# Side work of an attention block cut into smaller TensorE pieces, and the softmax denominators started earlier

## The chip, the cores and the metric

The kernel runs on one core of one Trainium2 chip. The metric is the device time of one execution in microseconds (us); each kernel's time is the median of its runs. The profile is one execution of the same program on the same kind of chip. TensorE is PE (matmuls) and PEld (its weight loads), VectorE is DVE, ScalarE is ACT, GpSimd is POOL, SyncE is SP.

## The reference

Eight frames of 2048 nodes with 256 channels go through one masked attention block with eight heads of 32 channels, two residual layer norms, a feed-forward layer, and an outer residual layer norm. All is float32.

```python
qkv = einsum('fnc,ck->fnk', x, w_qkv);  q, k, v = split(qkv, 3)      # 8 heads of 32
scores = einsum('fnhd,fmhd->fhnm', q, k) / sqrt(32)
attn = softmax(where(adj > 0, scores, -1e9), axis=-1)
t = einsum('fhnm,fmhd->fnhd', attn, v)
y = layernorm(x + t) * g1 + b1
z = layernorm(y + relu(y @ w1 + b1s) @ w2 + b2) * g2 + b2n
out = layernorm(x + z)                                              # x: the block's input
```

## The kernel before

**The tiling.** Scores are computed transposed: keys lie on the 128 partitions, queries along the row. Four heads make a group `g`, 512 queries a chunk `qc`, 128 keys a block `mb`. One *item* is (frame, chunk, group, block): four heads of 128 keys by 512 queries. A frame has 4 x 2 x 16 = 128 items, the kernel 1024. A run of 16 items (all blocks of one chunk and group) is called a *round* here.

**One item.** `scores` (L207) makes four matmuls of 32 rows that run side by side (L215) into two PSUM pairs out of three; two VectorE adds (L218) put the mask on them and leave them in SBUF as a tile `p` of 128 x 2048; `exponentials` (L221) is one ScalarE instruction in place (L222); `values` (L226) makes four matmuls of 32 columns side by side (L234) that add to one PSUM bank over the 16 blocks. The main loop (L513 to L540) is unrolled: at step t it emits first the side work that is due (`advance`, L428), then the exponentials of item t+1, the scores of item t+2 (`LEAD = 2`), the values of item t, and `add_up` of item t. This is TensorE's program order: side work, scores, values.

**The sums of the exponentials.** The softmax denominators need the sum of 16 `p` tiles. `add_up` (L249) does most of it off TensorE. `POOLED` names seven blocks that GpSimd adds into the first one (six adds, L256). `MOVED` names two chains of four blocks; each is added into the chain's first tile by a 1 MiB accumulating DMA (L253), which GpSimd issues. `ALONE` is a block that stays as it is. That leaves four tiles, and `denominator` (L280) multiplies each by ones on TensorE (L292): 4 heads side by side for each tile, all four tiles adding to one bank. It starts `SUM = 4` steps after the round's last item. Then the bank is copied, transposed (L299) and inverted.

**The side work.** Everything but scores and values is written as generators in a list `fill` that is sorted by due step: `turn` (transposes of x and the query projection), `project` (key and value projection through `channels`, L169, and the matmuls of L197), `denominator`, `outcome` (the division and the accumulating load of the residual), `tail` (L333: layer norms `norm`, L259, and `feed_forward`, L386). Two of the eight PSUM banks belong to neither score pair; one of them holds the running values, the other is for side work. A generator yields `BANK` before each use of that bank, a positive number to wait that many steps, and `INPUTS`, `TURNED` or `ROOM` to wait for a buffer. `advance(t, 1)` gives out one bank per step, in the order of the due steps; it isn't called at a round's first block. A job that got the bank emits all matmuls of the bank at once: 4 records for a projection of 128 x 512 (each float32 matmul shows as two records), 16 for a value projection, 16 for two tiles of `denominator`.

Of the kernel before, what the change touches and what calls it, by code (L numbers as in the profile page):

```python
# [26 lines left out]

SUM_MIN = 1e-25
SUM_MAX = 1e19
BANK, TURNED, ROOM, INPUTS = -1, -2, -3, -10  # L30

MASKED = -57344.0
CODE = -5.0
# [22 lines left out]
def fast_path(ctx, tc, cst, x, adj, out, RS):  # L56
# [20 lines left out]
    ctx.enter_context(tc.manual_schedule())  # L77

    ident, identb, wqkv, w1s, w2s = cst["ident"], cst["identb"], cst["wqkv"], cst["w1s"], cst["w2s"]
    state = {"pair": 0, "side": None, "turn": 0, "turned": False, "tails": 0}  # L80

    def score_pair():
        i = state["pair"]
# [57 lines left out]

    def queries(f, c, xT):
        for g in range(2):
            yield BANK
            QT[f, c, g] = channels(qp, "qT", xT, g * P)

    def turn_rows(xc, xT):
        for a in range(2):
# [17 lines left out]
        yield from queries(f, c, xT)  # L166
        give(xT)

    def channels(pool, name, xT, k0):  # L169
        ps = bank()  # L170
        for a in range(2):
            nc.tensor.matmul(ps, wqkv[:, a, k0:k0 + P], xT[:, a, :], start=(a == 0), stop=(a == 1))  # L172
        t = pool.tile([P, CH], F32, name=name)
        nc.scalar.copy(t, ps)
        return t

    def reload(f, c):
        while (f, c) not in XT:
# [7 lines left out]
    def project(f, c, g, xT=None):  # L186
        if xT is None:
            xT = yield from reload(f, c)
            while len(KT) < (2 * f + g) * NCK + c:
                yield 1  # L190
        yield BANK
        KT[f, c, g] = channels(kp, "kT", xT, C + g * P)
        yield BANK
        ps = bank()
        for j in range(TPC):
            for a in range(2):
                nc.tensor.matmul(ps[:, j * P:(j + 1) * P], xT[:, a, j * P:(j + 1) * P],  # L197
                                 wqkv[:, a, 2 * C + g * P:2 * C + (g + 1) * P], start=(a == 0), stop=(a == 1))
        v = vp.tile([P, TPC, P], F32, name="v")
        nc.scalar.copy(v, ps.rearrange("p (j c) -> p j c", c=P))  # L200
        V[f, c, g] = v
        give(xT)
# [36 lines left out]

    POOLED = (0, 3, 6, 8, 11, 13, 15)
    MOVED = ((1, 4, 7, 10), (2, 5, 9, 12))
    ALONE = 14

    ENDED = (13, 15)
    SUM = 4

    def add_up(item):  # L249
        f, qc, g, mb = item  # L250
# [8 lines left out]
    def norm(t):  # L259
        mv = small.tile([P, TPC, nc.vector.BN_AGGR_DIM], F32, name="mv")  # L260
        for j in range(TPC):
            st = small.tile([P, nc.vector.BN_STATS_DIM], F32, name="st")
            nc.vector.bn_stats(st, t[:, j, :])  # L263
            nc.vector.bn_aggr(mv[:, j, :], st)
            yield 1
        rs = small.tile([P, TPC], F32, name="rs")
        nc.gpsimd.tensor_scalar(rs, mv[:, :, 1], EPS, 1.0, op0=ALU.add, op1=ALU.mult)
        nc.gpsimd.tensor_tensor(rs, rs, cst["mhalf"], ALU.pow)  # L268
        nb = small.tile([P, TPC], F32, name="nb")
        nc.gpsimd.tensor_tensor(nb, mv[:, :, 0], rs, ALU.mult)  # L270
        nc.gpsimd.tensor_scalar(nb, nb, -1.0, 1.0, op0=ALU.mult, op1=ALU.mult)  # L271
        yield 2
        for j in range(TPC):
            nc.scalar.activation(t[:, j, :], t[:, j, :], AF.Identity, bias=nb[:, j:j + 1], scale=rs[:, j:j + 1])  # L274
            yield 1

    def rows(v):
        return v[:, None, :].to_broadcast([P, TPC, C])

    def denominator(f, qc, g):  # L280
        grp = (f, qc, g)
        terms = [PT.pop((f, qc, g, ALONE))] + [PT.pop((f, qc, g, chain[0])) for chain in MOVED + (POOLED,)]
        if (f, qc, g) == items[-1][:3]:
            terms[3:3] = [PT.pop((f, qc, g, b)) for b in ENDED]
        yield BANK
        ps = bank()
        for n, term in enumerate(terms):
            if n == 2:
                yield BANK
            for h in range(4):  # L290
                r = D * h
                nc.tensor.matmul(ps[r:r + D, :], cst["ones"], term[:, h, :], start=(n == 0), stop=(n == len(terms) - 1))  # L292
        dT = op.tile([P, CH], F32, name="dT")
        nc.scalar.copy(dT, ps)  # L294
        yield 1
        yield BANK
        ps = bank()
        for j in range(TPC):
            nc.tensor.transpose(ps[:, j * P:(j + 1) * P], dT[:, j::TPC], ident)  # L299
        if g == 0:  # L300
            RC[f, qc] = op.tile([P, TPC, H], F32, name="rc")
        rc = RC[f, qc]
        den = ps.rearrange("p (j c) -> p j c", c=P)[:, :, ::D]
        nc.vector.reciprocal(rc[:, :, 4 * g:4 * g + 4], den)
        nc.vector.tensor_tensor(RS[:, 0], RS[:, 0], den, ALU.add)
        nc.vector.tensor_tensor(RS[:, 1], RS[:, 1], den, ALU.min)
        if g == 1:
            begin = items.index((f, qc, g, LAST)) + SUM + 2
            start(begin, outcome(f, qc) if (f, qc) != (F - 1, NCK - 1) else finish(f, qc), begin)

    def outcome(f, qc):
        yield ROOM
        state["tails"] += 1
        xin = x[f, qc * CH:(qc + 1) * CH, :].rearrange("(p j) c -> p j c", p=P)
        y = yp.tile([P, TPC, C], F32, name="y")
        yield from divide(f, qc, y)
        nc.gpsimd.dma_start(y, xin, accum_op=ALU.add)
        begin = items.index((f, qc, 1, LAST)) + SUM + 2
        start(begin + 10, tail(f, qc, y, xin), begin + 26)

    def divide(f, qc, y):
        rc = RC.pop((f, qc))
# [43 lines left out]
                nc.scalar.activation(t[:, h + j, :], t[:, h + j, :], AF.Identity, bias=nb[:, j:j + 1], scale=rs[:, j:j + 1])  # L366

    def finish(f, qc):
        y = yp.tile([P, TPC, C], F32, name="y")
        xr, xb = state["rows"], take([P, TPC, C], F32)  # L370
        yield from divide(f, qc, y)
        nc.vector.tensor_tensor(y, y, xr, ALU.add)
        norm_halves(y)
        nc.vector.tensor_tensor(xb, xr, rows(cst["be2r"]), ALU.add)
        yield from feed_forward(y)
        z = y
        norm_halves(z)
        for h in range(0, TPC, 2):
            nc.vector.tensor_tensor(z[:, h:h + 2], z[:, h:h + 2], rows(cst["g2r"])[:, h:h + 2], ALU.mult)
            nc.vector.tensor_tensor(z[:, h:h + 2], z[:, h:h + 2], xb[:, h:h + 2], ALU.add)  # L380
        norm_halves(z)
        dst = out[f, qc * CH:(qc + 1) * CH, :].rearrange("(p j) c -> p j c", p=P)
        for h in range(0, TPC, 2):
            nc.sync.dma_start(dst[:, h:h + 2], z[:, h:h + 2])

    def feed_forward(y):  # L386
# [14 lines left out]
        for d in range(2):  # L401
            yield BANK
            ps = bank()
            for a in range(2):
                nc.tensor.matmul(ps, w1s[:, a, d * P:(d + 1) * P], yT[:, a, :], start=(a == 0), stop=(a == 1))  # L405
            nc.scalar.activation(hT[:, d, :], ps, AF.Relu, bias=cst["b1s"][:, d:d + 1], scale=1.0)
        state["turned"] = False
# [2 lines left out]
        for jj in range(0, TPC, 2):  # L410
            yield BANK
            ps = bank()
            for j in range(jj, jj + 2):
                for d in range(2):
                    nc.tensor.matmul(ps[:, (j - jj) * C:(j - jj + 1) * C], hT[:, d, j * P:(j + 1) * P], w2s[:, d, :],  # L415
                                     start=(d == 0), stop=(d == 1))
            nc.vector.tensor_tensor(z[:, jj:jj + 2, :], ps.rearrange("p (b c) -> p b c", c=C), z[:, jj:jj + 2, :], ALU.add)
# [7 lines left out]

    def advance(t, banks):  # L428
        inputs = True
        for e in list(fill):  # L430
            while e[0] <= t:
                if e[2] == BANK:
                    if not banks:
                        break
                    banks -= 1
                elif e[2] < INPUTS:
                    inputs = inputs and not any(u is not None for u in live[:INPUTS - e[2]])
                    if not inputs:
                        break
                elif e[2] == TURNED and state["turned"] or e[2] == ROOM and state["tails"] == 2:  # L440
                    break
                e[2] = next(e[1], None)
                if e[2] is None:
                    fill.remove(e)
                    break
                if e[2] > 0:
                    e[0] = t + e[2]

    items = [(f, qc, g, mb) for f in range(F) for qc in range(NCK) for g in range(2) for mb in range(MB)]
    LEAD = 2  # L450

# [61 lines left out]
    for t, (f, qc, g, mb) in enumerate(items):  # L513
# [3 lines left out]
            load_mask(f + (qc + 1) // NCK, (qc + 1) % NCK, mb // 2)  # L517
        if f + 1 < F:
            for what, *which in NEXT.get((2 * qc + g, mb), []):
                due = t + MB // 2 if what is turn else items.index((f + 1, 0, which[1], which[0] * TPC)) - LEAD - 1  # L520
                start(t, what(f + 1, *which), due)
        if t == len(items) - MB // 2:
            state["rows"] = take([P, TPC, C], F32)
            nc.sync.dma_start(state["rows"], x[f, qc * CH:(qc + 1) * CH, :].rearrange("(p j) c -> p j c", p=P))
        if mb:
            advance(t, 1)

        if t + 1 < len(items):
            exponentials(items[t + 1])
        if t + LEAD < len(items):  # L530
            nf, _, ng, nmb = items[t + LEAD]
            t0 = t
            while (nf, nmb // TPC, ng) not in V:
                advance(t0, 1)
                t0 += 1
            scores(items[t + LEAD])
        values(items[t])
        add_up(items[t])
        if mb == LAST:
            start(t + SUM, denominator(f, qc, g), t)  # L540
    t = len(items)
    state["side"] = None
    while fill:
        t += 1
        advance(t, 1)


@with_exitstack
# [233 lines left out]
```

## Time and profile before

The median is 3436.56 us (3432.72 to 3441.2); the profiled execution spans 3439.1 us at a granted TensorE clock of 0.99.

| stage | us | what runs |
|---|---|---|
| up to the first exponential | 59.7 | loads, masks, first projections |
| frame 0 | 442.2 | with the rest of the mask work |
| frames 1 to 6 | 414.2 to 419.6 each | steady |
| frame 7 | 382.3 | no next frame to project |
| after the last exponential | 57 | last denominators, last tail |

A frame is counted here from its first exponential to the next frame's. Divided by 128 items, a steady frame takes 3.25 us for an item. In the page, engines that are busy side by side each count fully; the row of a group gives the busy time, the mean of one instruction, and the idle time just before it with what ended it. A PE record's length is modelled and neighbours overlap, so distances from start to start are the better measure of what a matmul costs.

### The profile page before, as it was taken

Reading aid. Unit: us, or ns where it says so; the run is one execution under the profiler, and the core shown is the slowest. Engines: PE = TensorE matmul, PEld = TensorE weight load, DVE = VectorE, ACT = ScalarE, POOL = GpSimd, SP = SyncE. Lnnn points to the kernel's source line nnn. Section 1 sums busy time; section 2 is a strip of 40 time slices with the busy share of each in tenths; the row PEclk is TensorE's granted clock in tenths of the full one; section 3 lists DMA queues with packets and bytes.
Section 4 is the critical chain, followed back from the end, with each engine's and each line's share of the span. In section 5 each row is a group of like instructions: output and inputs, shape, how many; then the busy total and the mean of one; then the engine's idle time right before and its main releaser. Section 6 shows DMA issues by size and latency. Waiting matters only on the chain. (4 is left out here: it accounts for less than half of the span.)

```text
span 3439.1 us, 54435 instructions
## 1 busy us (share of the span) xinstructions
PE 3179.1 (92%) x22036; PEld 1038.5 (30%) x22036; DVE 2731.0 (79%) x3203; ACT 2426.5 (71%) x1937; POOL 2586.7 (75%) x1357
## 2 busy tenths in 40 slices
PE   6989999999999999999999999999999999998995
PEld 5222332223322233222332323223332223322222
DVE  4788768887788877888788887888768887689885
ACT  3677767776677767777677776777767777677774
POOL 0577768887688776888678876787777877788885
PEclk8999999999999999999999999999999999999998
DMA  8678768778678777778777777687776787777774
GB/s 309 149 156 173 173 161 174 158 159 200 142 167 184 154 180 153 163 172 181 170 154 170 161 175 178 141 180 172 164 179 140 160 187 167 169 158 154 151 162 99
DMA packets 149298, 575.99 MB, mean 167 GB/s; under 512 B 14608, under 2 KB 67344, under 8 KB 99888
## 3 DMA queue, kind: packets, MB, share of 16 engines
q0 software_dynamic: 64560, 435.85, 63.2%
q1 hardware_dynamic: 83664, 135.30, 11.4%
q8 instruction: 174, 2.85, 0.3%
q10 hardware_dynamic: 816, 1.31, 0.1%
q14 instruction: 84, 0.69, 0.1%
HBM read 131.99 MB, written 37.75 MB: 49 GB/s over the span
## 5 line engine op out<-in xcount | busy, mean ns | idle before, releaser
L218 DVE TENSOR_TENSOR p<-s,mask 128x1024 f32<-128x1024 f32 x2048 | 2410.0, 1219 | 568.5 <-PE s L215 343.9
L222 ACT ACTIVATE p<-p 128x2048 f32<-128x2048 f32 x1024 | 1956.6, 1911 | 484.6 <-DVE p L218 371.2
L256 POOL TENSOR_TENSOR p<-p 128x2048 f32<-128x2048 f32 x382 | 1851.8, 4898 | 385.9 <-ACT p L222 383.4
L215 PE MATMUL s<-qT,kT 32*128 32x512 f32 x8192 | 1169.8, 641 | 184.9 <-DVE p L218 174.6
L234 PE MATMUL x<-p,v 128*32 128x512 f32 x8192 | 1091.8, 605 | 2.3 <-ACT p L222 2.3
L253 POOL DMA_DIRECT2D p<-p x384 | 385.6, 1024 | 376.0 <-DMA p<-p 188.4
L215 PEld LDWEIGHTS s<-qT,kT 32*128 32x128 f32 x8192 | 320.5, 183 | 822.3 <-DVE p L218 756.2
L234 PEld LDWEIGHTS x<-p,v 128*32 128x32 f32 x8192 | 161.1, 108 | 780.1 <-issue 211.5
L172 PE MATMUL x<-in,wqkv 128*128 128x512 f32 x472 | 235.2, 621 | 14.7 <-DMA in<-xd 14.1
L292 PE MATMUL x<-p,ones 128*32 128x512 f32 x2064 | 244.9, 592 | 1.9 <-DMA p<-p 1.9
L274 ACT ACTIVATE y<-y,nb,rs 128x256 f32<-128x256 f32 x372 | 219.0, 590 | 7.1 <-POOL nb L271 7.1
L263 DVE BATCH_NORM_STATS2 st<-y 128x6 f32<-128x256 f32 x372 | 155.4, 418 | 0.0
L172 PEld LDWEIGHTS x<-in,wqkv 128*128 128x128 f32 x472 | 80.2, 189 | 170.9 <-issue 112.7
L294 ACT COPY dT<-x 128x512 f32<-128x512 f32 x64 | 37.4, 585 | 126.3 <-PE x L292 126.3
L415 PE MATMUL x<-w2s,hT 128*128 128x256 f32 x504 | 125.5, 392 | 0.1
L405 PE MATMUL x<-turned,w1s 128*128 128x512 f32 x248 | 123.0, 618 | 0.0
L197 PEld LDWEIGHTS x<-wqkv,in 128*128 128x128 f32 x896 | 104.2, 191 | 47.0 <-issue 41.1
L197 PE MATMUL x<-wqkv,in 128*128 128x128 f32 x896 | 114.9, 281 | 0.0
L292 PEld LDWEIGHTS x<-p,ones 128*32 128x32 f32 x2064 | 66.8, 110 | 156.4 <-issue 151.0
L415 PEld LDWEIGHTS x<-w2s,hT 128*128 128x128 f32 x504 | 90.6, 189 | 62.0 <-issue 50.3
L268 POOL TENSOR_TENSOR rs<-rs,mhalf 128x4 f32<-128x4 f32 x93 | 96.2, 1035 | 7.8
L200 ACT COPY v<-x 128x512 f32<-128x512 f32 x58 | 33.9, 585 | 93.6 <-PE x L197 93.6
(114 smaller groups left out, 1467.6 us busy)
## 6 DMA issues: line engine op xcount, KB each, us to landing
p<-p POOLq DMA_DIRECT2D x384, 1024.0 KB, 10.1
mask<-md SPq DMA_DIRECT2D x248, 128.0 KB, 6.2
y<-in_x_dram POOLq DMA_DIRECT2D x62, 512.0 KB, 6.1
in<-xd SPq DMA_DIRECT2D x59, 512.0 KB, 10.9
p<-in_adj_dram SPq DMA_DIRECT2D x16, 1024.0 KB, 9.6
out_dram<-y SPq DMA_DIRECT2D x31, 512.0 KB, 6.4
in<-in_x_dram SPq DMA_DIRECT2D x29, 512.0 KB, 10.4
xd<-in SPq DMA_DIRECT2D x28, 512.0 KB, 9.2
```

Source lines behind the costliest of these rows:

```text
L172: nc.tensor.matmul(ps, wqkv[:, a, k0:k0 + P], xT[:, a, :], start=(a == 0), stop=(a == 1))
L197: nc.tensor.matmul(ps[:, j * P:(j + 1) * P], xT[:, a, j * P:(j + 1) * P], wqkv[:, a, 2 * C + g * P:2 * C + (g + 1) * P], start=(a == 0), s ...
L215: nc.tensor.matmul(ps2[half][:, j, :], KT[f, mb // TPC, g][r:r + D, (mb % TPC) * P:(mb % TPC + 1) * P], QT[f, qc, g][r:r + D, :], start=Tr ...
L218: nc.vector.tensor_tensor(pt[:, 2 * half:2 * half + 2, :], ps, MK[f, qc, mb // 2][:, mb % 2, None, :].to_broadcast([P, 2, CH]), ALU.add)
L222: nc.scalar.activation(PT[item], PT[item], AF.Exp, scale=1.0 / math.sqrt(D))
L234: nc.tensor.matmul(O[grp][r:r + D, :], V[f, mb // TPC, g][:, mb % TPC, r:r + D], PT[item][:, h, :], start=(mb == 0), stop=(mb == LAST))
L253: nc.gpsimd.dma_start(PT[f, qc, g, chain[0]], PT.pop(item), accum_op=ALU.add)
L256: nc.gpsimd.tensor_tensor(first, first, PT.pop(item), ALU.add)
L263: nc.vector.bn_stats(st, t[:, j, :])
L274: nc.scalar.activation(t[:, j, :], t[:, j, :], AF.Identity, bias=nb[:, j:j + 1], scale=rs[:, j:j + 1])
L292: nc.tensor.matmul(ps[r:r + D, :], cst["ones"], term[:, h, :], start=(n == 0), stop=(n == len(terms) - 1))
L415: nc.tensor.matmul(ps[:, (j - jj) * C:(j - jj + 1) * C], hT[:, d, j * P:(j + 1) * P], w2s[:, d, :], start=(d == 0), stop=(d == 1))
```

## The change

It has five parts.

1. **Pieces.** A job that holds the bank may now yield `MORE` (or `HOLD`) between its matmuls. It stays the bank's holder and goes on at the next step, where no other job gets a bank. `channels`, the value projection, both feed-forward layers and the products of `denominator` are divided in this way, one half or one tile for each step. The aim is to put the same TensorE work on more steps, a smaller piece on each.
2. **Urgency.** If any job that waits for a bank is due within `SOON = 8` steps, the holder's `MORE` pieces are all emitted at once, as before. A `HOLD` (ahead of the third tile of `denominator`) isn't hurried in this way. A round's last step empties the bank.
3. **The sums.** `ALONE` is the last block, 15, in place of 14, so that it goes to TensorE without any add. The chains become (1, 4, 7, 11) and (2, 6, 9, 13), the GpSimd sum (0, 3, 5, 8, 10, 12, 14). `denominator` starts 2 steps after the round's last item (`SUM = 2`, block 1 of the next round) in place of 4, and takes block 15, chain 1, the GpSimd sum and chain 2 in this order.
4. **Due steps.** `denominator` and `outcome` are due at once; projections are due 7 steps earlier.
5. **Tails.** A tail starts 7 steps after its own accumulating load was issued, in place of at a fixed step; `norm` waits a step less ahead of and behind its activations; the last chunk's `finish` waits for room as the others do.

```diff
-BANK, TURNED, ROOM, INPUTS = -1, -2, -3, -10
+BANK, MORE, HOLD, TURNED, ROOM, INPUTS = -1, -2, -3, -4, -5, -10
...
-    def channels(pool, name, xT, k0):
+    def channels(store, pool, name, key, xT, k0):
+        yield BANK
         ps = bank()
         for a in range(2):
+            if a:
+                yield MORE
             nc.tensor.matmul(ps, wqkv[:, a, k0:k0 + P], xT[:, a, :], start=(a == 0), stop=(a == 1))
...
         for j in range(TPC):
+            if j == TPC // 2:
+                yield MORE
             for a in range(2):
                 nc.tensor.matmul(ps[:, j * P:(j + 1) * P], xT[:, a, j * P:(j + 1) * P],
...
-    POOLED = (0, 3, 6, 8, 11, 13, 15)
-    MOVED = ((1, 4, 7, 10), (2, 5, 9, 12))
-    ALONE = 14
-    ENDED = (13, 15)
-    SUM = 4
+    POOLED = (0, 3, 5, 8, 10, 12, 14)
+    MOVED = ((1, 4, 7, 11), (2, 6, 9, 13))
+    ALONE = 15
+    ENDED = (12, 14)
+    SUM = 2
...
-        terms = [PT.pop((f, qc, g, ALONE))] + [PT.pop((f, qc, g, chain[0])) for chain in MOVED + (POOLED,)]
+        terms = [PT.pop((f, qc, g, ALONE))] + [PT.pop((f, qc, g, chain[0])) for chain in (MOVED[0], POOLED, MOVED[1])]
...
         for n, term in enumerate(terms):
-            if n == 2:
-                yield BANK
+            if n:
+                yield HOLD if n == 2 else MORE
             for h in range(4):
...
-        begin = items.index((f, qc, 1, LAST)) + SUM + 2
-        start(begin + 10, tail(f, qc, y, xin), begin + 26)
+        start(state["step"] + 7, tail(f, qc, y, xin), state["step"] + 24)
...
+    def resume(e, t):
+        e[2] = next(e[1], None)
+        state["holder"] = e if e[2] in (MORE, HOLD) else None if state["holder"] is e else state["holder"]
+        if e[2] is None:
+            fill.remove(e)
+        elif e[2] > 0:
+            e[0] = t + e[2]
+
-    def advance(t, banks):
+    def advance(t, free=True, finish=False):
+        state["step"] = t
         inputs = True
+        if state["holder"]:
+            free = False
+            resume(state["holder"], t)
         for e in list(fill):
-            while e[0] <= t:
+            while e[2] is not None and e[0] <= t and e is not state["holder"]:
                 if e[2] == BANK:
-                    if not banks:
+                    if not free:
                         break
-                    banks -= 1
+                    free = False
...
+        late = any(e[2] == BANK and e[0] <= t and e[3] <= t + SOON for e in fill)
+        while state["holder"] and (finish or late and state["holder"][2] == MORE):
+            resume(state["holder"], t)
+
+    SOON = 8
...
-                due = t + MB // 2 if what is turn else items.index((f + 1, 0, which[1], which[0] * TPC)) - LEAD - 1
+                due = t + MB // 2 if what is turn else items.index((f + 1, 0, which[1], which[0] * TPC)) - LEAD - 8
...
         if mb:
-            advance(t, 1)
+            advance(t, finish=mb == LAST)
...
         if mb == LAST:
-            start(t + SUM, denominator(f, qc, g), t)
+            start(t + SUM, denominator(f, qc, g), 0)
```

The feed-forward layers get the same `yield MORE` between their halves.

More of the change, by code (lines that the diff above doesn't have):

```diff
@@ L79, in fast_path @@
     ident, identb, wqkv, w1s, w2s = cst["ident"], cst["identb"], cst["wqkv"], cst["w1s"], cst["w2s"]
-    state = {"pair": 0, "side": None, "turn": 0, "turned": False, "tails": 0}
+    state = {"pair": 0, "side": None, "turn": 0, "turned": False, "holder": None, "step": 0, "tails": 0}
     def score_pair():
@@ L143, in queries @@
         for g in range(2):
-            yield BANK
-            QT[f, c, g] = channels(qp, "qT", xT, g * P)
+            yield from channels(QT, qp, "qT", (f, c, g), xT, g * P)
     def turn_rows(xc, xT):
@@ L167, in turn @@
         give(xT)
-    def channels(pool, name, xT, k0):
+    def channels(store, pool, name, key, xT, k0):
+        yield BANK
         ps = bank()
         for a in range(2):
+            if a:
+                yield MORE
             nc.tensor.matmul(ps, wqkv[:, a, k0:k0 + P], xT[:, a, :], start=(a == 0), stop=(a == 1))
-        t = pool.tile([P, CH], F32, name=name)
-        nc.scalar.copy(t, ps)
-        return t
+        store[key] = pool.tile([P, CH], F32, name=name)
+        nc.scalar.copy(store[key], ps)
     def reload(f, c):
@@ L190, in project @@
                 yield 1
-        yield BANK
-        KT[f, c, g] = channels(kp, "kT", xT, C + g * P)
+        yield from channels(KT, kp, "kT", (f, c, g), xT, C + g * P)
         yield BANK
@@ L273, in norm @@
         for j in range(TPC):
+            if j:
+                yield 1
             nc.scalar.activation(t[:, j, :], t[:, j, :], AF.Identity, bias=nb[:, j:j + 1], scale=rs[:, j:j + 1])
-            yield 1
     def rows(v):
@@ L281, in denominator @@
         grp = (f, qc, g)
-        terms = [PT.pop((f, qc, g, ALONE))] + [PT.pop((f, qc, g, chain[0])) for chain in MOVED + (POOLED,)]
+        terms = [PT.pop((f, qc, g, ALONE))] + [PT.pop((f, qc, g, chain[0])) for chain in (MOVED[0], POOLED, MOVED[1])]
         if (f, qc, g) == items[-1][:3]:
-            terms[3:3] = [PT.pop((f, qc, g, b)) for b in ENDED]
+            terms[2:2] = [PT.pop((f, qc, g, b)) for b in ENDED]
         yield BANK
@@ L287, in denominator @@
         for n, term in enumerate(terms):
-            if n == 2:
-                yield BANK
+            if n:
+                yield HOLD if n == 2 else MORE
             for h in range(4):
@@ L307, in denominator @@
         if g == 1:
-            begin = items.index((f, qc, g, LAST)) + SUM + 2
-            start(begin, outcome(f, qc) if (f, qc) != (F - 1, NCK - 1) else finish(f, qc), begin)
+            begin = items.index((f, qc, g, LAST)) + SUM + 4
+            start(begin, outcome(f, qc) if (f, qc) != (F - 1, NCK - 1) else finish(f, qc), 0)
     def outcome(f, qc):
@@ L368, in finish @@
     def finish(f, qc):
+        yield ROOM
         y = yp.tile([P, TPC, C], F32, name="y")
@@ L404, in feed_forward @@
             for a in range(2):
+                if a:
+                    yield MORE
                 nc.tensor.matmul(ps, w1s[:, a, d * P:(d + 1) * P], yT[:, a, :], start=(a == 0), stop=(a == 1))
@@ L413, in feed_forward @@
             for j in range(jj, jj + 2):
+                if j > jj:
+                    yield MORE
                 for d in range(2):
@@ L441, in advance @@
                     break
[L442 to L447, printed above, removed]
+                resume(e, t)
+        late = any(e[2] == BANK and e[0] <= t and e[3] <= t + SOON for e in fill)
+        while state["holder"] and (finish or late and state["holder"][2] == MORE):
+            resume(state["holder"], t)
+    SOON = 8
     items = [(f, qc, g, mb) for f in range(F) for qc in range(NCK) for g in range(2) for mb in range(MB)]
@@ L533, in fast_path @@
             while (nf, nmb // TPC, ng) not in V:
-                advance(t0, 1)
+                advance(t0, finish=True)
                 t0 += 1
@@ L544, in fast_path @@
         t += 1
-        advance(t, 1)
+        advance(t, finish=True)
 @with_exitstack
```

## The prediction, made before the changed kernel was run

> **What bounds the kernel now.** I read first the page's busy shares and groups, then the same for stretches of one frame, then the order of time inside one item.
>
> From the page, the shares, the groups that matter and the issue row of the accumulating DMAs:
>
> ```profile
> PE 3179.1 (92%) x22036; PEld 1038.5 (30%) x22036; DVE 2731.0 (79%) x3203; ACT 2426.5 (71%) x1937; POOL 2586.7 (75%) x1357
> ...
> L218 DVE TENSOR_TENSOR p<-s,mask 128x1024 f32<-128x1024 f32 x2048 | 2410.0, 1219 | 568.5 <-PE s L215 343.9
> ...
> L256 POOL TENSOR_TENSOR p<-p 128x2048 f32<-128x2048 f32 x382 | 1851.8, 4898 | 385.9 <-ACT p L222 383.4
> L215 PE MATMUL s<-qT,kT 32*128 32x512 f32 x8192 | 1169.8, 641 | 184.9 <-DVE p L218 174.6
> ...
> L253 POOL DMA_DIRECT2D p<-p x384 | 385.6, 1024 | 376.0 <-DMA p<-p 188.4
> ...
> L292 PE MATMUL x<-p,ones 128*32 128x512 f32 x2064 | 244.9, 592 | 1.9 <-DMA p<-p 1.9
> ...
> p<-p POOLq DMA_DIRECT2D x384, 1024.0 KB, 10.1
> ```
>
> TensorE is the fullest engine, and nearly all its idle time lies before the scores (L215), in wait for a VectorE add to free a PSUM pair. The sums cost TensorE almost nothing: 1.9 us of idle before L292 in the whole run.
>
> Busy time of each engine in a steady frame and in the last one:
>
> ```profile
> 1333.00:1747.00 414.00, 393.20 (x2721) 126.52 (x2720) 335.48 (x393) 300.80 (x240) 324.13 (x169) 1.00 0.76 168
> 3000.00:3382.00 382.00, 342.67 (x2494) 97.75 (x2496) 332.51 (x390) 283.69 (x208) 316.62 (x167) 1.00 0.74 154
> ```
>
> The columns are PE, PEld, DVE, ACT, POOL, clock, DMA share. In a steady frame PE is busy for 393.2 of 414.0 us: a change of order alone can win at most 20.8 us a frame. Where they lie shows in the timeline:
>
> ```profile
> 1005.12 1.14 PE L215 MATMUL s<-qT,kT 32*128 32x512 f32 x8 [0.41 <-DVE p L218]
> ...
> 1006.19 1.07 PE L234 MATMUL x<-p,v 128*32 128x512 f32 x8
> ...
> 1007.19 1.98 PE L405 MATMUL x<-turned,w1s 128*128 128x512 f32 x4
> ...
> 1009.10 1.14 PE L215 MATMUL s<-qT,kT 32*128 32x512 f32 x8
> ...
> 1010.17 1.06 PE L234 MATMUL x<-p,v 128*32 128x512 f32 x8
> ```
>
> Values, a whole side job, scores, values: 1010.17 - 1006.19 = 3.98 us, without a gap on PE. A step without side work is held by VectorE instead: two adds 1.13 us apart and a turn-round, with the 0.41 us PE gap of the first row. I took each step from values to values for items 100 to 899: 242 steps without side work last 2.62 us (the common one 2.54); whole jobs 3.98 to 4.05 (two tiles of ones-products 3.78); single transposes (0.66 us of PE) 2.65 to 2.86. So **a step lasts the longer of 2.07 us plus its side work, and about 2.55 us**, and the kernel alternates between overfull and underfull steps.
>
> **What the Trainium skill says.** "TensorE: Matmul & The Clock Gate" ("Step-by-step: what each phase is for") has matmuls stay in program order, with only weight loads pulled ahead. The rows above agree: values follow scores follow side work, and a ones-product that waits would hold all behind it. "DMA: Bandwidth & Descriptors" ("Rules for kernel authors") asks an accumulating DMA to wait for the earlier one on the same bytes; the 188.4 us before L253 are that. Its fit ("Anatomy of one DMA", 2.0 us + bytes / 436e3) would give 4.4 us for 1 MiB; the issue row has 10.1, and that is used. "PSUM — Partial Sum Buffer" ("The four PSUM rules") keeps an accumulation group's state in the bank until the next opening matmul there: a group held over steps needs no matmul more. No run shows this yet; I cost it at nothing.
>
> **Part 1 and 2, pieces.** Price of a half: in a whole projection the first of four records starts 1.914 us before the scores; the last one starts 0.522 us before them, records of one matmul are 0.429 apart. So half takes 0.429 + 0.522 = 0.951, and its step 0.996 (values to side work) + 0.951 + 1.071 (scores to values) = **3.02 us**, above VectorE's 2.55 (2.81 when a norm's 0.55 us lies in the step: also hidden). The total is unchanged, since 2 x 0.951 is 1.914 within 0.02. For ones-products: values to products 0.883, one tile 0.947 (the pair's 1.830 less the 0.883 of its first), 1.071: 2.90.
>
> A division turns a whole job's step and an idle one into two halves: 3.98 + 2.62 - 2 x 3.02 = 0.56 us won; ones-products 3.78 + 2.62 - 2 x 2.90 = 0.60. The lower end of this price is nothing (the idle step was already needed by VectorE), the upper 0.6.
>
> How many? Before, a steady frame wants 88 banks in 120 steps with `advance`; 32 and the 8 first blocks stay empty. After, following the new rules through one frame, the 32 banks of transposes stay single and the other 56 become 112 pieces: 144 in all. 6 of the 120 steps stay empty for lack of a ready job, so 114 carry work and 144 - 114 = 30 steps take two pieces through urgency. 26 jobs a frame are really divided: 20 x 0.56 + 6 x 0.60 = 14.8 us, of the 20.8 there are. Over all frames I count 30, 23, five times 26, and 22: 205 divisions x 0.57 = **117 us**.
>
> **Part 3, the sums.** They keep 6 adds of 4.9 us and 6 issues of 1.02 in a round; nothing is removed. But the four tiles are asked for sooner. Queued behind a waiting L292 are the scores, the values and so VectorE and ScalarE; what is lost is lost whole.
> GpSimd's tile: exponential 14 ends 2.0 us after values 13 begin; the product comes 0.9 us after values 18. Five steps of about 3 less 1.1 leave 13.7 us. In the trace the last add (block 15) ends 10.2 us after its exponential in the mean, 14.1 at most (frames 1 to 6): safe.
> Chain 2's tile, last moved block 13: in six of eight rounds urgency puts it in the same step, one product after GpSimd's tile, so 17.6 us after exponential 13. Before, the last moved block (12) also stood right behind a GpSimd add; it was issued 7.1 us after its exponential and landed 9.6 later: 16.7 in the mean, 10.9 to 21.8. The excess of each of those 48 sums over 17.6 is 0.77 us in the mean, over 18.6 (two rounds have a step more) 0.47. The estimate is 64 rounds x 0.62 = **40 us** of new waiting. The bounds: 18 us at a limit of 19.5, 124 at 15.5. More than half is in the rounds at the fourth place of a frame, at 21.0 in the mean.
> Two neighbours in chain are now 3 steps apart twice (4 to 7, 6 to 9) where it was three times: GpSimd's 188.4 us of waits get a little less, off the path.
>
> **Part 4 and 5.** Earlier due steps only order the list; the latest value projection would still stand 4 steps ahead of its first scores. The norm's activations come up to three steps sooner on ScalarE, which has 113 us idle in a frame. The last stretch of 57 us keeps its work: chain 2 lands some 13 us after exponential 13, by when exponential 15, its values and five products (0.95 each) have run. Nothing, plus or minus 5.
>
> **Sum.** 3436.6 - 117 + 40 = **3360 us**.
>
> **Rivals.**
> - *Clean gain*, chance 0.33: the adds move closer to their exponentials, since the GpSimd blocks are now evenly spaced, and L292 doesn't wait. 3436.6 - 117 = 3320. For it: 1.9 us of waiting today. Against: today's limits are wider.
> - *My forecast*, 0.42: 3360.
> - *VectorE joins in*, 0.13: a half step with a norm or a residual add becomes 3.2 us instead of 3.02, since the score pairs turn round with less slack. Then 410 half steps lose 0.18, 74 us: 3436.6 - 117 + 74 + 10 = 3404.
> - *The sums become the bound*, 0.12: GpSimd is busy for 324 us of a frame that would shrink to 399, with waits on landings on top (24.5 us in the steady frame); bursts from the tails push the last issue 2 us later in each round. 124 us and a little more: 3436.6 - 117 + 130 = 3450, slower.
>
> The range takes in the clean case and reaches to the edge of the slow one: 3315 to 3435. Faster by over 0.3% (below 3426): 0.33 + 0.42 + 0.11 of the third, 0.86. Within 0.3%: 0.02 of the third and 0.03 of the last, 0.05. Slower: the other 0.09 of the last.
>
> **What would show it.** PE's busy time stays near 3180 with a share of 94 to 95%. The idle of L215 on VectorE falls from 175 to below 90 us. Steps with one half of L405 or L172 last 3.02, not 3.2. The idle before L292 rises from 1.9 to about 40, released by the landing of `p<-p`, most of it in one round of eight. I am wrong if L292's idle stays near zero (then nearer 3320) or passes 100, or if the half steps are longer than 3.1.

## The result, and the profile after

| kernel | median, us | ratio to the kernel before, 95% interval |
|---|---|---|
| before (timed beside it) | 3435.72 | 1 |
| after | 3482.92 (3481.93 to 3489.76) | 1.0140 (1.0121 to 1.0158) |

The change makes the kernel 1.4% slower; 2.2% faster was forecast. From the page of the changed kernel, the rows that answer to those shown before (scores are now L217, their masks L220, chains L255, ones-products L295):

```profile
PE 3233.7 (93%) x22036; PEld 1034.5 (30%) x22036; DVE 2736.3 (78%) x3203; ACT 2432.5 (70%) x1937; POOL 2584.0 (74%) x1357
...
L220 DVE TENSOR_TENSOR p<-s,mask 128x1024 f32<-128x1024 f32 x2048 | 2409.8, 1218 | 581.3 <-PE s L217 374.2
...
L217 PE MATMUL s<-qT,kT 32*128 32x512 f32 x8192 | 1184.8, 648 | 91.4 <-DVE p L220 87.8
...
L255 POOL DMA_DIRECT2D p<-p x384 | 399.0, 1069 | 135.3 <-DMA p<-p 65.8
...
L295 PE MATMUL x<-p,ones 128*32 128x512 f32 x2064 | 263.4, 605 | 28.6 <-DMA p<-p 25.0
```

The idle time before the scores has halved, from 184.9 to 91.4 us: the pieces do fill underfull steps. Yet VectorE waits longer for scores than before (374.2 for 343.9), PE is busy 55 us longer with the same 22036 matmuls, and 28.6 us of idle stand before the ones-products. The rest shows only in the waits. From the list of who waited for whom (us in total, times, longest):

```profile
DVE y L331 <- DMA out_dram<-y: 60.6, 14, 9.0
...
PE x L330 <- DVE y L331: 53.6, 14, 8.7
...
PE x L295 <- DMA p<-p: 25.0, 18, 5.1
```

The first two rows are new. L331 is the division, a VectorE operation that writes into a `y` buffer; it waits 14 times for the *store* of an earlier tail. In the kernel before, the same operation waits for nothing (the last figure is its idle time):

```profile
L329 DVE TENSOR_TENSOR y<-x,rc 128x512 f32<-128x512 f32 x62 | 42.4, 684 | 0.0
```

One such place in the timeline, round 0 of frame 3 (matmuls, VectorE, and the store on SyncE's queue):

```profile
1362.19 0.34 SPq L348 DMA_DIRECT2D out_dram<-y  x1
...
1369.24 1.06 PE L236 MATMUL x<-p,v 128*32 128x512 f32 x8
...
1373.40 0.69 DVE L331 TENSOR_TENSOR y<-x,rc 128x512 f32<-128x512 f32 x1 [4.43 <-DMA out_dram<-y]
1374.01 2.34 DVE L220 TENSOR_TENSOR p<-s,mask 128x1024 f32<-128x1024 f32 x2
...
1374.15 0.75 PE L330 MATMUL x<-ident,oT 128*128 128x128 f32 x4 [3.85 <-DVE y L331]
...
1375.28 1.84 PE L217 MATMUL s<-qT,kT 32*128 32x512 f32 x8 [0.39 <-DVE p L220]
```

A tail stores its last rows and, in the same step, counts as ended; the next chunk's division, which had been kept back by `ROOM`, may start. But only two `y` buffers exist and the store takes 11 us to land. The adds of the scores stand behind the division in VectorE's program and start only after it (1374.01), and TensorE's scores wait for them (1375.28). The step takes 7.81 us, where a division's usual step takes 2.75. Afterwards the matmuls themselves are slow: the scores take 1.84 us in place of 1.14. The granted clock (last but two of the columns) says why:

```profile
1375.60:1379.00 3.40, 3.40 (x17) 0.29 (x9) 3.19 (x4) 1.91 (x1) 1.75 (x2) 0.50 1.01 210
1379.00:1382.00 3.00, 3.00 (x25) 2.12 (x25) 0.52 (x1) 0.97 (x2) 3.00 (x2) 1.00 1.01 202
```

The Trainium skill names this ("TensorE: Matmul & The Clock Gate", "HAM oscillation — how this bites in real kernels": no idle gaps over about 3.4 us). This place agrees: behind PE's 3.85 us without work the clock is half for 3.4 us. As a border, 3.4 us doesn't agree with these traces: ahead of seven other dips in the changed kernel the longest gap between PE's records is 2.06 to 2.73 us, while four gaps of 2.00 to 2.46 us in the kernel before have no dip behind them. Dips come 22 times in the changed kernel (168.8 us in sum, the slow start and end included; most last 3.4 us, some 6.8 or 10.2), 4 times before (69.3 us).

Where the forecast went in the six steady frames, from the durations of their 768 steps:

| us for each frame | forecast | measured |
|---|---|---|
| jobs cut in two, at the forecast's price | -14.8 | -14.8 (not a measured gain: the pieces counted in the trace, at that price) |
| a half step is 3.12 us, not 3.02 (value projection 3.15); 40 of them | 0 | +4.0 |
| steps with a division (L331): 3.81 us in the mean, 2.86 before; 8 | 0 | +7.6, and 0.5 in the step behind |
| steps with ones-products: 3.12 us for one tile (2.90), 4.17 for two (3.78); 11.7 and 10.2 | +5.0 | +6.6 |
| sum | -9.8 | +3.9 (416.3 to 420.2) |

Differences of other kinds of steps, each up to about 1.5 us a frame, nearly cancel and are left out.

Of the 6.6 us, only 3.1 are steps that wait for a tile, behind the fourth and, once, the sixth round. Another 2.7 come from a wait of a different kind, behind the sixth round in the five other frames:

```profile
1656.29 0.60 ACT L278 ACTIVATE y<-y,nb,rs 128x256 f32<-128x256 f32 x1 [3.54 <-POOL nb L273]
1656.80 1.89 ACT L224 ACTIVATE p<-p 128x2048 f32<-128x2048 f32 x1
...
1658.74 1.84 PE L236 MATMUL x<-p,v 128*32 128x512 f32 x8 [2.07 <-ACT p L224]
```

A norm's activation on ScalarE waits for its small GpSimd operations, which stand here behind a 4.9 us add of the sums (from 1649.40). The exponential stands behind the activation, and TensorE's values wait for the exponential. ScalarE waits in this way for 33.9 us in the changed kernel, 7.1 us in the kernel before.

Frame 7 takes 405.9 us, 23.5 more than before: one of its steps with a division alone lasts 13.5, and projections that were done in frame 6 before now lie in it. By the same shift fewer lie in frame 0, which is 5.2 us shorter. The stretch after the last exponential grows from 57 to 64 us.

### The profile page after: what moved, and what is told of

Read it like the earlier page. It is cut to its first block, busy times and chain, and to the rows that moved or that the text cites. A ratio compares the mean times of both kernels' runs of the same rounds, so it can differ in the third digit from the quotient of the medians.

```text
span 3487.9 us, 54434 instructions
## 1 busy us (share of the span) xinstructions
PE 3233.7 (93%) x22036; PEld 1034.5 (30%) x22036; DVE 2736.3 (78%) x3203; ACT 2432.5 (70%) x1937; POOL 2584.0 (74%) x1357
## 4 chain that ended last, share of the span: by engine, by line
PE 59%; DMA 12%; DVE 9%; POOL 6%; ACT 4%; issue 3%; DVEq 0%; POOLq 0%; ACTq 0%
PE s L217 21%; PE x L236 17%; DMA p<-p 8%; DVE p L220 7%; PE x L295 5%; PE x L174 4%; DMA out_dram<-y 4%; PE x L422 3%; PE x L199 3%; PE x L410 3%; POOL p L258 2%; ACT p L224 2%; PE x L302 1%; ACT y L278 1%; DVE st L265 1%
## 5 line engine op out<-in xcount | busy, mean ns | idle before, releaser
L220 DVE TENSOR_TENSOR p<-s,mask 128x1024 f32<-128x1024 f32 x2048 | 2409.8, 1218 | 581.3 <-PE s L217 374.2
L217 PE MATMUL s<-qT,kT 32*128 32x512 f32 x8192 | 1184.8, 648 | 91.4 <-DVE p L220 87.8
L236 PE MATMUL x<-p,v 128*32 128x512 f32 x8192 | 1104.2, 611 | 10.4 <-ACT p L224 10.4
L217 PEld LDWEIGHTS s<-qT,kT 32*128 32x128 f32 x8192 | 323.6, 185 | 677.4 <-DVE p L220 600.6
L255 POOL DMA_DIRECT2D p<-p x384 | 399.0, 1069 | 135.3 <-DMA p<-p 65.8
L295 PE MATMUL x<-p,ones 128*32 128x512 f32 x2064 | 263.4, 605 | 28.6 <-DMA p<-p 25.0
L174 PE MATMUL x<-in,wqkv 128*128 128x512 f32 x472 | 254.9, 636 | 0.5 <-DMA in<-xd 0.5
L278 ACT ACTIVATE y<-y,nb,rs 128x256 f32<-128x256 f32 x372 | 216.5, 590 | 34.1 <-POOL nb L273 33.9
L269 POOL TENSOR_SCALAR rs<-mv 128x4 f32<-128x4 f32 x93 | 17.9, 193 | 155.5 <-DVE mv L266 150.5
L295 PEld LDWEIGHTS x<-p,ones 128*32 128x32 f32 x2064 | 65.7, 112 | 195.5 <-issue 138.6
L341 POOL TENSOR_TENSOR y<-y,g2r 128x1024 f32<-128x1024 f32 x31 | 76.4, 2463 | 54.8 <-ACT y L278 54.8
## 6 DMA issues: line engine op xcount, KB each, us to landing
in<-in_x_dram SPq DMA_DIRECT2D x29, 512.0 KB, 10.2
```

What stands on the lines that cost most here:

```text
L217: nc.tensor.matmul(ps2[half][:, j, :], KT[f, mb // TPC, g][r:r + D, (mb % TPC) * P:(mb % TPC + 1) * P], QT[f, qc, g][r:r + D, :], start=Tr ...
L220: nc.vector.tensor_tensor(pt[:, 2 * half:2 * half + 2, :], ps, MK[f, qc, mb // 2][:, mb % 2, None, :].to_broadcast([P, 2, CH]), ALU.add)
L236: nc.tensor.matmul(O[grp][r:r + D, :], V[f, mb // TPC, g][:, mb % TPC, r:r + D], PT[item][:, h, :], start=(mb == 0), stop=(mb == LAST))
L255: nc.gpsimd.dma_start(PT[f, qc, g, chain[0]], PT.pop(item), accum_op=ALU.add)
```

## The experiments

Theory A: the pieces are a real gain, which new waits for transfers eat up: the wait for `y`, and the wait for the sums. Theory B: the pieces themselves cost more than the idle steps they fill. Ratios are to the kernel before, timed beside each.

**e1_third_y: a third `y` buffer.**

```diff
-    mkp = ... bufs=MB // 2 + 1    qp = ... bufs=2 * NCK + 2    yp = ... bufs=2
+    mkp = ... bufs=MB // 2        qp = ... bufs=2 * NCK + 1    yp = ... bufs=3
```

> The changed kernel with a third buffer for y (one buffer less for queries and one for masks pays for the room). Theory A: the change loses by new waits, not by the pieces; about 8 us a frame is the division's VectorE operation in wait for the store of the tail that had just ended to leave its y buffer, with all of TensorE behind it. Then the steps with a division fall from 3.81 to about 2.8 us in the mean, the 60 us of VectorE waiting for the output store go, and the time is about 3420. Theory B: the pieces themselves cost more than the idle steps they fill (more changes of matmul form). Then the stall's end only moves the wait, and the time stays above 3465.

Measured: 3415.23 us, 0.9908 (0.9891 to 0.9924). From the groups of this run, the division and the ones-products:

```profile
L295 PE MATMUL x<-p,ones 128*32 128x512 f32 x2064 | 262.8, 602 | 29.0 <-DMA p<-p 22.5 <-POOL p L258 5.8 <-DVE y L424 0.5
...
L331 DVE TENSOR_TENSOR y<-x,rc 128x512 f32<-128x512 f32 x62 | 42.2, 680 | 0.0
```

The idle before L331 is gone, that before L295 is as it was, and the step with a division lasts 2.76 us in the mean. With one buffer the slower kernel becomes a faster one; B falls.

**e2_tail_due_16: the tail hurried instead.** The same wait taken away in another way, with two buffers.

```diff
-        start(state["step"] + 7, tail(f, qc, y, xin), state["step"] + 24)
+        start(state["step"] + 7, tail(f, qc, y, xin), state["step"] + 16)
```

> The changed kernel with a tail due 16 steps after its start of reckoning in place of 24, so that its pieces are hurried sooner and it ends 9 or more steps ahead of the next division but one. Two y buffers as before. Theory A: the wait for y goes as with a third buffer, 364 half steps are left of 410, which gives back some 9 us: about 3430. Theory B: above 3465.

Measured: 3427.20 us, 0.9939 (0.9922 to 0.9956). The division's wait falls from 60.6 to 7.8 us. Two unlike edits that remove the same wait both turn the loss into a gain, each within 5 us of the time expected of it (the kernel before ran 10 us slower beside these two than beside the changed kernel, so the gain by ratio is larger than expected).

**e3_sum_4: the later start of the denominators.**

```diff
-    SUM = 2
+    SUM = 4
```

> The changed kernel with the denominators started 4 steps after a round's last item again (SUM = 4), all else as changed. Theory A: the waits ahead of the ones-products (about 6 us a frame, 28.6 us of idle on PE in the profile and as much again in lower clock and late scores behind it) go, but divisions come 2 steps later and, by the rules of the list, nearer to the end of the tail whose buffer they need in three chunks of four in place of two: the wait for y grows. Together 3440 to 3475. If the early start were the whole cause, about 3430 or less with the wait for y unchanged. Theory B: within 10 us of the changed kernel.

Measured: 3490.24 us, 1.0118 (1.0097 to 1.0139). The idle before the ones-products is 0.0; the division now waits 20 times:

```profile
DVE y L331 <- DMA out_dram<-y: 67.3, 20, 7.4
```

By the time alone B would hold too: it is within 10 us of the changed kernel, and 15 us above A's range. The waits are those that A named: one went and the other grew (from 60.6 us), so that neither shows alone.

**e5_third_y_sum_4: both waits removed** (third `y`, `SUM = 4`).

> The changed kernel with both suspected waits taken away: a third buffer for y (as in e1_third_y), and the denominators started 4 steps after a round's last item. Theory A (two separate waits hide a real gain of the pieces): no wait ahead of the ones-products and none for y; e1_third_y less the 40 us of waiting that it still had ahead of its ones-products: about 3380. Theory C (the early start of the denominators also wins something, so that the later start costs what the waits gave): 3405 to 3425.

Measured: 3397.48 us, 0.9847 (0.9829 to 0.9864): the best version of the study, 1.5% faster than the kernel before. A steady frame of it, and its ones-products:

```profile
1313.00:1722.00 409.00, 397.39 (x2717) 126.28 (x2708) 334.95 (x391) 300.78 (x242) 325.47 (x169) 1.00 0.77 170
```

```profile
L295 PE MATMUL x<-p,ones 128*32 128x512 f32 x2016 | 246.1, 592 | 0.0
```

PE is busy for 397.4 of 409.0 us: 11.6 us of idle where there were 20.8. The time lies between A and C. From the third-`y` kernel to this one the gain is 0.6%, about 21 us, half of what A gave the wait for the sums. The early start had probably won something too: VectorE waits 3.5 us for free `p` tiles in e1_third_y, 15.2 us here.

**e8_third_y_sum_3: `SUM = 3`** with the third `y`.

> e1_third_y with the denominators started 3 steps after the round's last item: between the two. Theory A: a step of about 3 us more takes the excess of the last chain from about 1 us to about 0.3 us a round: 3385 to 3400, between e5_third_y_sum_4 and e1_third_y.

Measured: 3402.22 us, 0.9858 (0.9840 to 0.9876): 2 us above the range that A gave, and as good as 4 within the intervals.

**e7_third_y_old_sums: the old chains** in the best version (`POOLED`, `MOVED`, `ALONE`, `ENDED` and the order of the tiles as before).

> e5_third_y_sum_4 with the chains, the lone block 14 and the order of the tiles of the kernel before: the pieces, due steps and tails alone, with a third y. Theory A: at the later start the choice of the chains is worth nothing on TensorE, since neither set is waited for: within 10 us of e5_third_y_sum_4, about 3380. If the new chains save GpSimd waiting that counts, this one is slower by more than that.

Measured: 3401.01 us, 0.9859 (0.9840 to 0.9877): no difference in time. It shows what the new chains are good for. VectorE's wait for a free `p` tile, first with the old chains, then with the new ones:

```profile
DVE p L220 <- DMA p<-p: 68.0, 28, 4.0
```

```profile
DVE p L220 <- DMA p<-p: 15.2, 7, 4.1
```

They free tiles sooner, but with these due steps VectorE could wait. With the old due steps the chains matter (e12_pieces_and_tails below).

**e4_no_pieces:** the changed kernel with every job whole.

```diff
-        while state["holder"] and (finish or late and state["holder"][2] == MORE):
+        while state["holder"] and (finish or state["holder"][2] == MORE):
```

> The changed kernel with every divided job put out whole at once (a holder that says MORE always goes on), so that only the new sums, the due steps and the tails' timing are left of the change. Theory A: about 205 divisions at 0.36 us are lost (some 75 us), the tails are short again and the wait for y goes (60 us), the sums' early start still costs: 3455 to 3490. Theory B: the time comes back to that of the kernel before or below it, 3437 at most.

Measured: 3565.65 us, 1.0351 (1.0331 to 1.0371), far above both theories. Whole jobs take two tiles in a step, block 15 and the first chain at block 1 of the next round, the GpSimd sum and the second chain at block 2. The total, and one place of it:

```profile
L295 PE MATMUL x<-p,ones 128*32 128x512 f32 x2064 | 265.0, 619 | 84.8 <-DMA p<-p 84.7
```

```profile
1525.19 1.04 PE L295 MATMUL x<-p,ones 128*32 128x512 f32 x8
...
1531.18 1.94 PE L295 MATMUL x<-p,ones 128*32 128x512 f32 x8 [4.95 <-DMA p<-p]
```

This wait stands at block 1, between the first and the second tile. In the whole run 71.6 of the 84.8 us stand there, for the first chain, which no expectation had named; 13.1 us are for the second chain at block 2.

In its steady frames the steps with ones-products last 4.86 us in the mean in place of 3.79, 103 us for six frames; all other steps together are 8 us shorter than before.

**e6_no_pieces_sum_4:** the same with `SUM = 4`.

> The changed kernel with all jobs whole, as in e4_no_pieces, and the denominators started 4 steps after the round again. What is left of the change is the new chains, the new order of the tiles, the due steps and the tails' timing. Theory A: e4_no_pieces was slow only because whole jobs ask for the last two sums at block 2 (a step sooner than the pieces do); with the later start the wait ahead of the ones-products falls from 84.7 us to under 10, and the time is that of the kernel before within 12 us: 3435 to 3458. Rival D: the new chains or due steps cost by themselves: above 3470.

Measured: 3508.78 us, 1.0174 (1.0155 to 1.0194), 50 us above what A expected, and in the range of rival D. Two waits for transfers stand in its groups, and none for `y`:

```profile
L295 PE MATMUL x<-p,ones 128*32 128x512 f32 x2064 | 249.0, 593 | 14.5 <-DMA p<-p 14.4
...
L174 PE MATMUL x<-in,wqkv 128*128 128x512 f32 x472 | 245.2, 644 | 30.5 <-DMA in<-xd 30.5
...
L331 DVE TENSOR_TENSOR y<-x,rc 128x512 f32<-128x512 f32 x62 | 42.2, 680 | 0.0
```

The first is all for the second chain, now at block 4. The second is the reload of the transposed input, awaited by a projection. The steps with projections are 27 us longer in six frames than before and those with ones-products 23 us, the half clock behind each gap included, which is nearly all of the loss in these frames (54 us). Why the reload is met too early was not tried; that the projections' earlier due steps put them ahead of other jobs is the likely reason. Against the best version, which differs by the pieces and by the third `y` (which this one doesn't wait for), the pieces are worth 3.3% here.

**e10_new_sums_alone**, on the kernel before: new chains, order and `SUM = 2`, jobs whole.

> The kernel before with part 3 alone: the new chains, block 15 alone, the new order of the tiles and the start 2 steps after the round's last item, all jobs whole. Theory A: whole jobs ask for the GpSimd sum and the second chain at block 2 of the next round, one to two steps sooner than the pieces do, so TensorE waits ahead of the ones-products as in e4_no_pieces (84.7 us of idle, about as much again behind it): 1.02 to 1.035 of the kernel before. If the slowness of e4_no_pieces came from the due steps or the tails: within 1.01.

Measured: 3639.45 us, 1.0555 (1.0535 to 1.0576); 141.2 us of idle before the ones-products, and their steps 158 us longer in six frames. The direction is A's, the size nearly double. Of the idle 50.6 us are for the first chain at block 1 and 84.8 for the second at block 2. The requests come at the same blocks as in e4_no_pieces; that the tails' GpSimd work lies differently to the sums here is a possible reason and wasn't tried.

**e9_pieces_alone**, on the kernel before: parts 1 and 2 without the rest.

> The kernel before with the pieces and their urgency alone (parts 1 and 2): chains, start and order of the sums, due steps, tails and two y buffers as before. Theory A: the pieces are the gain and the other parts the loss. By the rules of the list some 410 half steps at 3.12 us take the place of 205 whole and 205 idle ones, 82 us less; the last division of a frame comes within 2 steps of the tail that frees its buffer, which costs up to 20 us: 0.976 to 0.986 of the kernel before. Theory F (the pieces need the other parts, for instance the earlier due steps, to gain): no faster than 0.995.

Measured: 3451.65 us, 1.0012 (1.0003 to 1.0021). A's expectation fails and F's holds: alone the pieces win nothing. From the waits of this run:

```profile
DVE p L220 <- DMA p<-p: 45.1, 30, 3.1
...
DVE st L265 <- DMA y<-in_x_dram: 36.2, 8, 6.3
```

and one of the eight places of the second row:

```profile
1067.15 0.43 DVE L265 BATCH_NORM_STATS2 st<-y 128x6 f32<-128x256 f32 x1 [4.27 <-DMA y<-in_x_dram]
...
1068.95 2.09 PE L217 MATMUL s<-qT,kT 32*128 32x512 f32 x8 [5.01 <-DVE p L220]
```

A tail starts at its fixed step, though the division and its accumulating load now come later; VectorE stops for the load, and TensorE after it. The first row is a shortage of `p` tiles; it can hardly be what takes the gain, since e7_third_y_old_sums waits longer for them (68.0 us) and is 1.4% faster than the kernel before. Besides, two jobs fall in one step (5.85 or 6.00 us) twice a frame, where a projection was forced because it was nearly too late. With parts 4 and 5 and a third `y` added to these pieces, which is e7_third_y_old_sums, the gain appears (0.9859).

**e11_y3_sum4_old_due: old due steps** in the best version (`- LEAD - 1` in place of `- LEAD - 8`).

> e5_third_y_sum_4 with the projections due as late as before (1 step in place of 8 ahead of their first scores less two). Theory A: what e5 still waits for ahead of the projections (half steps of channels last 3.22 us in the mean, 3.12 in the median) is the reload of the transposed input, which an earlier due step asks for before it has landed; with the old due steps that goes: 5 to 12 us below e5_third_y_sum_4. Otherwise the same within 4 us.

Measured: 3420.71 us, 0.9911 (0.9895 to 0.9928), 0.64% above the best version, not below it: my reason was wrong. The earlier due steps are worth some 22 us; with the old ones a forced step of 6.00 us stands in each frame again, and half steps of projections last up to 8.59 us.

**e12_pieces_and_tails:** the third `y`, the tails' timing and the due denominators added to the pieces-alone kernel, the projections' due steps old.

> e9_pieces_alone (0.12% slower than the kernel before) with the tails timed by their own loads, denominators and divisions due at once, and the third y buffer; the sums' chains and start and the projections' due steps stay as before. In e9 VectorE waits 36.2 us for the tails' own loads, with the scores behind it. If the fixed start of the tails is what took that kernel's gain, this one lies at 0.990 to 0.994: the 22 us that the old due steps cost in e11_y3_sum4_old_due above e7_third_y_old_sums (0.986). If the tails' timing is worth nothing, it stays above 0.998.

Measured: 3487.05 us, 1.0121 (1.0100 to 1.0143): not the gain that was expected, and slower than e9_pieces_alone itself, which neither case named. The wait for the tails' loads is gone, but:

```profile
PE x L151 <- DMA in<-in_x_dram: 58.6, 6, 10.4
```

Once in each of six frames the first transposes of a new input meet its load before it has landed; these steps last 12.8 to 14.5 us. Steps of this kind are 71 us longer in six frames than before, so without them this kernel would be near 0.99; that is arithmetic, but e11_y3_sum4_old_due bears it out. The two differ in nothing but the chains, the lone block and the order of the tiles, and e11, at 0.9911, has no such wait. The load of frame 1 is issued at the same time in both (563.4 and 563.7 us); it lands 8.1 us later in e11 and 24.6 us later here, where a 1 MiB transfer of a chain is issued at the same moment (563.63) and not some 5 us after it (568.34). So the old chains cost nothing with the new due steps (e7) and 2.1% with the old ones; with the old chains the old due steps cost 2.7% (e7 to this one).

## Why the prediction was wrong

**The step that failed is the price of a piece.** The prediction counted TensorE's time alone ("the lower end of this price is nothing"), put parts 4 and 5 at "nothing, plus or minus 5", and had no term for what longer jobs do to the buffers: "Earlier due steps only order the list", it said, and of the tails no word beyond the activations and the end. The traces of frames 1 to 6 show the missing term. Before, a tail's store comes 56 steps after its chunk's first division, and the next division but one, which needs the same `y` buffer of the two, 8 steps after that store. In the changed kernel the store comes after 55 to 64 steps, and in three chunks of four that division follows it by 1 or 3 steps. `ROOM` counts a buffer free at the issue of its store, not at its landing, which took 11 us in the place shown.

Neither side brings this wait alone. Without pieces, but with parts 3 to 5 (e4, e6), the division follows by 10 steps and L331 waits 0.0 us; with the pieces and none of the other parts (e9) it follows by 4 to 9 steps and waits 0.0 us too. The list had in it all that was needed (when each tail ends, when the next division but one starts), and I didn't set them side by side. A third buffer is worth 2.3% (1.0140 to 0.9908), about 80 of the 123 us between forecast and result. No rival had it: the one that ended slower named the sums.

**The price of a half** was mis-sized. I took 0.429 us as the distance of the first two records after a change of matmul form; in the whole job as in the half it is 0.533, and the last record stands 0.523 before the scores: 1.056, not 0.951. A half step of the changed kernel, values to values 3.12 us:

```profile
1382.00 1.07 PE L236 MATMUL x<-p,v 128*32 128x512 f32 x8
...
1382.99 1.13 PE L174 MATMUL x<-in,wqkv 128*128 128x512 f32 x2
...
1384.05 1.14 PE L217 MATMUL s<-qT,kT 32*128 32x512 f32 x8
...
1385.12 1.06 PE L236 MATMUL x<-p,v 128*32 128x512 f32 x8
```

So each such cut costs 0.20 us of PE (2 x 1.056 less 1.914), and a cut of ones-products about 0.1; 205 cuts make some 36 of the 55 us by which PE's busy time grew, where it was to stay near 3180. The prediction had named half steps over 3.1 us as a sign of being wrong. The check "2 x 0.951 is 1.914 within 0.02" looked like a proof and was a coincidence: it left the entry out of both halves.

**What held.** The number of pieces of each kind agrees with the trace to within one a frame. The scores' idle time in wait for VectorE was to fall from 175 to below 90 us; it is 87.8. Half steps have the same length in nearly all places (median and 90th percentile 3.12), so the rival of VectorE joining in is out.

**The sums** held in direction, in part by luck. 40 us of waiting were forecast, mostly for the landing, mostly at the fourth round; PE idles 28.6 us before the ones-products, 25.0 of it for the landing, and the fourth round leads. But 10.0 us of it stand ahead of the first chain, which the prediction didn't look at. Two of its readings were loose as well: six rounds at 0.77 and two at 0.47 make 0.70 in the mean and 44 us, not 0.62 and 40; and the GpSimd sum was called safe with 14.1 us at most against 13.7 allowed (3.2 us of the idle are for it). In steps the waits for tiles make 3.1 us a frame for 5.0 forecast. Starting the denominators later, which removes the wait, won only 21 us.

**Left open**: the 7 us at the end (64 to 68 us after the last exponential in eight of the ten kernels with pieces, but 58 in e11 and e12, and 53 to 57 in those without); why the first chain lands late in e4 and e10; what the wait of the norms for GpSimd costs, which no run removes by itself; and why the new sums alone cost 5.5%.

## What to carry to other kernels

Cutting side work into pieces stretches every job made of them: before costing it, lay the new life of each buffer beside the next request for it, and count a buffer free at the landing of its store, not at its issue. A job that starts by a step count meets its transfer too early as soon as anything else moves; in this kernel nearly every timing variant moved the place where an in-order engine met a transfer in flight, and the longer of these meetings cost 2 to 12 us each. When two changes belong together, undoing one tells little alone: the pieces are worth 3.3% in one setting and nothing in another.

## What was unexpected of the hardware

A gap of under 4 us on TensorE is paid nearly one and a half times: the clock is at 0.5 for 3.4 us behind it, which takes up to 1.7 us more (an estimate, half of the 3.4), and scores that take 1.14 us take up to 2.09. Gaps of 2.06 to 2.73 us had such a dip behind them in seven places. A 512 KB store took 11 us to land (median 8.9 us in the changed kernel, 6.4 before), and the same 512 KB load, issued at the same time, 8.1 us in one kernel and 24.6 in another that differs only in the chains of its accumulating DMAs. So when a buffer changes hands is set by the traffic of the moment.
